# Edge attention on one core: 36 rows a group fetched row by row, by two queues, in place of 8 by one

## The chip, the cores and the metric

The kernel runs on one core of a Trainium2 chip. Times are device microseconds (us) of that core. TensorE (PE) multiplies matrices, VectorE (DVE) and ScalarE (ACT) work on tiles, GpSimd (POOL) and the sync engine (SP) mostly start transfers here. Each engine works through its own list of instructions in order; semaphores tie the lists together. SP and ScalarE can start ordinary DMAs; GpSimd starts gathers, which are DMAs whose source rows are read from a table of indices.

## The reference

The computation is one graph-attention layer with a residual and two norms. There are 12500 nodes of 128 values and 212500 edges, sorted by destination:

```python
Q = (x @ WQ).reshape(N, H, dh); K = (x @ WK)...; V = (x @ WV)...
Eh = (edge_attr @ WE).reshape(-1, H, dh)
score = K[src] * Q[dst] / jnp.sqrt(jnp.float32(dh)) * Eh
score = jnp.exp(jnp.clip(score.sum(-1, keepdims=True), -5.0, 5.0))
msg = V[src] * score
wV = jax.ops.segment_sum(msg, dst, num_segments=N)
Z = jax.ops.segment_sum(score, dst, num_segments=N)
h = x + (wV / (Z + ATTN_EPS)).reshape(N, D)
h = batch_norm(h); out = layer_norm(x + h)
```

H is 8 and dh 16. `K[src]` and `V[src]` are random reads: every edge needs one row of K and V, 256 floats or 1 KB.

## The kernel before, in words

**Table.** First the kernel computes K and V of all nodes and writes them to a table in DRAM, `kvd`, one 1 KB row a node. While the table is being written, GpSimd gathers rows of `x` itself for the first eight groups.

**Groups.** The edges are cut into 1661 tiles of 128 edges, and eight tiles make a group, so that there are 208 groups. For each tile, one gather by GpSimd (line 221) brings 128 rows of `kvd`, one a partition, into a column of the group's slot. Nine slots are used in turn. When VectorE has made the messages of a group (`message`, line 663), its slot is free, and the gathers of the group nine later are queued for GpSimd.

**One group's work.** VectorE multiplies the K rows with the transposed product of Q and edge features (`products`, line 639), sums by head (`scores`, 647), clips (657), and after ScalarE's exp (658, 659) multiplies V with it (`message`, 663). It also builds one-hot matrices (541 to 551) with which TensorE sums the messages by destination (680). ScalarE copies results out of TensorE's accumulators: the edge features (595), the sums (685), the nodes' new values (710), and Q in three bf16 parts, the first of them at line 569 (`q_hi`), the second at 576 (`q_mid`). VectorE computes what remains of Q after the first part at line 573 (`q_rest`), just ahead of `message` in its list.

**Order.** The order on every engine is the order of the calls in the loop over groups, written out by hand. In a pass g it begins: load the edge features of group g + 4 on SP (506; it waits until TensorE is done with the features of group g + 1, since there are three buffers), on some passes load a block of relative destinations on SP (404), then `fetch_rows(g)`, then `q_hi(g + 3)`, `products(g)`, and so on. ScalarE's list around the pass's beginning is thus: `q_mid` of the pass before, then `q_hi`, then the two exps.

**Rows.** In some groups the last of the eight columns is not gathered by GpSimd. Its 128 rows are fetched one at a time by SP: `fetch_rows` (lines 269 to 284) loads the byte offsets of a pass's rows from an SBUF tile (`row_ids`) into registers (274) and starts one DMA of 1 KB for each row (281) into a tile of its own, `byrow`, of which there are two. `row_plan` (61 to 71) decides which groups: eight rows a pass from pass 8 on make a full tile every 16 passes, and it is used two passes after its last row was started (`ROW_LAG`). There are 12 such groups, the first is 25. Before such a column is read, VectorE waits on a semaphore that counts its rows (`rows_there`). A group with such a column splits lines 639, 647 and 663 into two instructions. The offsets' nodes are loaded in pass 2 (`load_row_ids`, 264) and made byte offsets on VectorE in pass 4.

Of the kernel before, what the change touches and what calls it, by code (L numbers as in the profile page):

```python
# [10 lines left out]
U8 = mybir.dt.uint8  # L11
I32 = mybir.dt.int32
# [3 lines left out]
ET = mybir.EngineType  # L16

P = 128
# [4 lines left out]
U = 4  # L23
# [4 lines left out]
EARLY = 3  # L28
RUN = 64
ROWS = P  # L30
FIRST_ROW = 8
LATE = 8
ROW_LAG = 2
SP_ROWS = 8
WORDS = 4
RQ = 4
NSEM = 6
# [40 lines left out]
def gnn_kernel(  # L78
# [31 lines left out]
    consts = ctx.enter_context(tc.tile_pool(name="consts", bufs=1))  # L110
# [129 lines left out]

    by_row, fill = {}, {}
    row_loads = []
    n = SP_ROWS
    row_tiles = row_plan(usizes)
    tot = len(row_tiles) * P
    cols = -(-n // WORDS) * WORDS
    full_rows = tot // n
    blocks = -(-tot // (P * n))
    for q in range(0, full_rows, P):
        row_loads.append((0, q // P * cols, min(P, full_rows - q), n, q * n))  # L250
    if tot % n:
        row_loads.append((full_rows % P, full_rows // P * cols, 1, tot % n, full_rows * n))
    for q in range(-(-tot // n)):
        fill[FIRST_ROW + q] = q
    by_row.update({g: None for g in row_tiles})
    rows_in = [tc.alloc_semaphore(f"rows_in{i}") for i in range(NSEM)]
    row_ids = consts.tile([P, blocks * cols], I32, name="row_ids")
    nc.vector.memset(row_ids, 0)
    kvb = kvd.bitcast(U8).rearrange("n d -> (n d)")

# [1 line left out]
        return [(a, b - 1), (b - 1, b)] if g in by_row and b == G else [(a, b)]  # L262

    def load_row_ids():
        for p, c, m, w, at in row_loads:
            nc.scalar.dma_start(row_ids[p:p + m, c:c + w], bass.AP(
                tensor=rsrc.tensor, offset=rsrc.offset + at, ap=[[n, m], [1, w]]))

    def fetch_rows(g):
        if g not in fill:  # L270
            return
        q = fill[g]
        c = q // P * cols
        _, offs = nc.values_load_multi_w_load_instructions(
            row_ids[q % P:q % P + 1, c:c + cols], engines=(ET.SP,), min_val=0, max_val=(N - 1) * 8 * P,
            skip_runtime_bounds_check_because="node ids")
        for r, off in zip(range(q * n, min(q * n + n, tot)), offs):
# [3 lines left out]
            d = nc.sync.dma_start(by_row[k][r % P:r % P + 1, 0, :].bitcast(U8), kvb[ds(off, 8 * P)].unsqueeze(0))  # L281
# [69 lines left out]
    def within(f, g):  # L351
        return f(g) if 0 <= g < NG else None
# [405 lines left out]
    for q in range(NQ):  # L758
# [13 lines left out]
        k = q - first_step  # L772
# [70 lines left out]
    for g in range(NG - 2):  # L843
        within(load, g + 4)
        within(load_rel, g + 5)
        if (g + 6) % RQ == 0 and (g + 6) // RQ in quads:
            load_quad((g + 6) // RQ)
        fetch_rows(g)
        within(q_hi, g + 3)
        within(products, g)  # L850
        within(q_lo, g + 2)
# [13 lines left out]
        else:  # L865
            left = len(queued)
# [35 lines left out]
        if g == LATE - 2:  # L902
# [3 lines left out]
    g = last - 1  # L906
# [4 lines left out]
                           skip_runtime_bounds_check_because="a count")]  # L911
# [321 lines left out]
```

## Time and profile before

| what | value |
|---|---|
| median of 3 runs | 2134.45 us (2132.48 to 2135.73) |
| profiled execution, its own time | 2128.07 us |
| its span | 2126.3 us |
| PE busy | 1714.8 us (81%) |
| DVE busy | 1591.9 us (75%) |
| POOL busy | 1594.3 us (75%) |
| ACT busy | 671.6 us (32%) |
| gathers from `kvd` | 1585 |
| single rows fetched by SP | 1536 |

Durations come from the profiled execution. The span is the time from its first to its last instruction; the time of a run has 1.8 us more around it. Busy times leave out instructions that only load registers, wait, or start a DMA, so that SP has no busy time at all, and ScalarE's busy time holds no DMA issue.

### The profile page before, as it was taken

How to read it: one execution, taken by the hardware profiler on the slowest of the kernel's cores; microseconds unless marked ns; L12 is line 12 of the kernel's file. 1: busy time of each engine (PE TensorE's matmuls, PEld its weight loads, DVE VectorE, ACT ScalarE, POOL GpSimd, SP SyncE). 2: the span in 40 equal slices, each digit the busy share in tenths (PEclk: the TensorE clock that was granted, in tenths of full speed). 3: DMA queues.
4: the chain of work that ended last, by engine and by line, in shares of the span. 5: the costliest groups of instructions: out<-in, count | busy, mean ns of one | idle time of the engine just before them, and what ended most of it. 6: DMA issues, size and time to landing. Idle time of an engine off the chain costs nothing. (4 is left out here: it accounts for less than half of the span.)

```text
span 2126.3 us, 34575 instructions
## 1 busy us (share of the span) xinstructions
PE 1714.8 (81%) x9414; PEld 1106.1 (52%) x9414; DVE 1591.9 (75%) x3593; ACT 671.6 (32%) x2688; POOL 1594.3 (75%) x1685
## 2 busy tenths in 40 slices
PE   8889999877777777877777778778778777777787
PEld 7566565544444444545444545545445444544456
DVE  4559999777777777777777777777777777777787
ACT  3344343323223223223223223223223232222225
POOL 7777777777777777777777777777777777777775
PEclk9999999998999999998999999888998998988898
DMA  9856666565565565565565565565565565565574
GB/s 311 277 183 206 193 197 195 175 178 171 169 178 169 169 180 167 170 182 169 166 183 164 171 183 168 168 184 167 166 185 165 167 186 165 166 186 165 170 236 126
DMA packets 175392, 386.62 MB, mean 182 GB/s; under 512 B 37518, under 2 KB 91831, under 8 KB 175191
## 3 DMA queue, kind: packets, MB, share of 16 engines
q0 software_dynamic: 78128, 212.05, 33.9%
q1 hardware_dynamic: 92900, 169.50, 25.8%
q10 hardware_dynamic: 4163, 2.78, 0.5%
q8 instruction: 78, 1.28, 0.2%
q14 instruction: 123, 1.01, 0.1%
HBM read 364.57 MB, written 19.63 MB: 181 GB/s over the span
## 5 line engine op out<-in xcount | busy, mean ns | idle before, releaser
L221 POOL DMA_INDIRECT slot<-kvd,srcs x1585 | 1506.0, 950 | 484.0 <-issue 402.8
L639 DVE TENSOR_TENSOR slot<-slot,ps_t 128x512 f32<-128x512 f32 (+1 forms) x410 | 274.7, 678 | 421.2 <-DMA slot<-kvd,srcs 383.8
L621 PE MATMUL ps_t<-ident,wt 128*128 128x128 f32 x1661 | 285.7, 315 | 356.0 <-DVE wt L613 353.0
L680 PE MATMUL ps_a<-msg,oh 128*128 128x136 f32 (+1 forms) x3322 | 526.2, 297 | 1.9 <-DVE msg L663 1.9
L621 PEld LDWEIGHTS ps_t<-ident,wt 128*128 128x128 f32 x1661 | 214.8, 161 | 530.8 <-issue 460.7
L680 PEld LDWEIGHTS ps_a<-msg,oh 128*128 128x128 f32 (+1 forms) x3322 | 426.8, 171 | 81.7 <-issue 54.4
L658 ACT ACTIVATE ps_m<-s 128x64 f32<-128x64 f32 (+1 forms) x209 | 47.5, 227 | 1093.4 <-DVE s L657 1009.4
L588 PE MATMUL ps_e<-ea,w_e 128*128 128x512 f32 x832 | 390.6, 591 | 0.7 <-ACT wt L595 0.7
L613 DVE TENSOR_TENSOR wt<-wt,ps_q 128x512 f32<-128x512 f32 x416 | 264.6, 677 | 2.2 <-PE ps_q L603 2.2
L663 DVE TENSOR_TENSOR msg<-slot,ps_m 128x1024 f32<-128x1024 f32 (+3 forms) x209 | 246.9, 1183 | 0.4 <-ACT ps_m L658 0.3
L647 DVE TENSOR_REDUCE s<-slot 128x64 f32<-128x1024 f32 (+2 forms) x208 | 246.7, 1187 | 0.1
L595 ACT ACTIVATE wt<-ps_e 128x512 f32<-128x512 f32 x416 | 233.4, 618 | 11.5 <-PE ps_e L588 11.2
L603 PE MATMUL ps_q<-ot,q 64*128 64x512 bf16 x1248 | 212.6, 456 | 0.0
L588 PEld LDWEIGHTS ps_e<-ea,w_e 128*128 128x128 f32 x832 | 142.6, 190 | 100.4 <-issue 98.5
L541 DVE TENSOR_TENSOR oh<-ps_m,rel_i 128x512 f32<-128x512 f32 x208 | 142.0, 683 | 11.1 <-PE ps_a L680 11.1
L569 ACT ACTIVATE q<-qs 128x128 bf16<-128x128 f32 x208 | 64.3, 309 | 220.1 <-PE ps_q L603 186.2
L705 PEld LDWEIGHTS ps_a<-ident,at 128*128 128x128 f32 x408 | 71.2, 218 | 111.5 <-issue 55.5
L705 PE MATMUL ps_a<-ident,at 128*128 128x128 f32 x408 | 114.2, 367 | 2.5 <-DVE relrow L395 2.3
L710 ACT ACTIVATE hx<-ps_a 128x64 f32 x408 | 88.3, 217 | 43.1 <-PE ps_a L680 32.1
L530 ACT ACTIVATE xw<-hx 128x64 f32 x416 | 88.1, 279 | 10.4 <-DMA hx<-xT 6.0
L603 PEld LDWEIGHTS <-q 64*128 64x128 bf16 x1248 | 48.9, 103 | 80.7 <-issue 64.1
L561 PE MATMUL ps_a<-w_q,xw 128*128 128x128 f32 x416 | 88.8, 299 | 0.6 <-ACT qs L565 0.4
(180 smaller groups left out, 1633.9 us busy)
## 6 DMA issues: line engine op xcount, KB each, us to landing
ea<-eaT SPq DMA_DIRECT2D x207, 512.0 KB
slot<-kvd,srcs POOLq DMA_INDIRECT x1585
byrow<-kvd SPq DMA_DIRECT2D x1536, 1.0 KB
rbq<-relT SPq DMA_DIRECT2D x94, 256.0 KB
kvd<-slot SPq DMA_DIRECT2D x12, 512.0 KB
kvd<-t SPq DMA_DIRECT2D x12, 512.0 KB
slot<-xT SPq DMA_DIRECT2D x24, 256.0 KB
out<-o SPq DMA_DIRECT2D x23, 256.0 KB
```

Of the source, the lines that this page charges most:

```text
L221: return nc.gpsimd.indirect_dma_start(out=out, out_offset=None, in_=table, in_offset=bass.IndirectOffsetOnAxis(ap=srcs[:, e:e + 1], axis=0))
L541: nc.vector.tensor_tensor(one, iota_ps[:, None, :].to_broadcast([P, n, P]), r[:, :n, None].to_broadcast([P, n, P]), op=OP.is_equal)
L588: nc.tensor.matmul(eh, w_e, EA[g][:, a:b, :].rearrange("p a b -> p (a b)"), start=True, stop=True)
L595: nc.scalar.activation(t[:, :(b - a) * P], EH[g][h], AF.Copy)
L603: nc.tensor.matmul(QE[g][h], Q3[g][r, k, :], OT[g][r, :(b - a) * P], start=(k == 0), stop=(k == 2))
L613: nc.vector.tensor_tensor(t, t, QE[g][h], op=OP.mult)
L621: nc.tensor.transpose(ps[:, j, :], WT[g][h][:, j * P:(j + 1) * P], ident)
L639: step = nc.vector.tensor_tensor(kv, kv, PW[g][i][:, c - a:d - a, :], op=OP.mult)
L647: step = nc.vector.tensor_reduce(SS[g][:, a:b, :], KV[g](a, b, 0).rearrange("p t (h d) -> p t h d", d=DH), axis=AX.X, op=OP.add)
L663: step = nc.vector.tensor_tensor(MSG[g][:, a:b, :P].rearrange("p t (h d) -> p t h d", d=DH), KV[g](a, b, P).rearrange("p t (h d) -> p t h ...
L680: nc.tensor.matmul(AGG[g][WN if j >= n else 0:], OH[g][j], MSG[g][:, j, :], start=(j == 0), stop=(j == n - 1))
L705: nc.tensor.matmul(ps, AT[g], ident, start=True, stop=False)
```

## The change

Each pass now fetches 36 rows in place of 8. SP starts 20 of them and ScalarE starts 16; ScalarE's come in the loop just ahead of `q_hi(g + 3)`. The first fetch is in pass 6 in place of 8. A tile of 128 rows is full every 3.56 passes: 55 groups (11, 15, 18, 22, ..., 203) have a column by rows in place of 12, and GpSimd issues 1542 gathers from `kvd` in place of 1585. The total of single rows is 7040 in place of 1536, over 196 passes (6 to 201).

Each engine loads its own offsets into its own registers: 20 words on SP in place of 8, and 16 words on ScalarE. `row_ids` becomes a tile of 128 x 72 words with two passes in a partition, and it is filled by five DMAs on ScalarE in place of two (two large ones and three for the remainder). Everything else in the loop stays in its place.

```diff
-FIRST_ROW = 8
+FIRST_ROW = 6
-SP_ROWS = 8
+SP_ROWS = 20
+ACT_ROWS = 16
...
-    full, n = sizes.count(U) // 2, SP_ROWS
+    full, n = sizes.count(U) // 2, SP_ROWS + ACT_ROWS
...
+    row_loads.append((0, 0, [[2 * n, pairs], [n, 2], [1, SP_ROWS]], 0, sp_step))
+    row_loads.append((0, act_at, [[2 * n, pairs], [n, 2], [1, ACT_ROWS]], SP_ROWS, act_step))
...
+    def offsets(q, et):
+        c, w, m = (0, sp_step, SP_ROWS) if et == ET.SP else (act_at, act_step, ACT_ROWS)
+        _, offs = nc.values_load_multi_w_load_instructions(
+            row_ids[q // 2:q // 2 + 1, c + q % 2 * w:c + (q % 2 + 1) * w], engines=(et,), min_val=0,
+            max_val=(N - 1) * 8 * P, skip_runtime_bounds_check_because="node ids")
+        return offs[:m]
+
-    def fetch_rows(g):
+    def fetch_rows(g, et, a, b):
         if g not in fill:
             return
-        q = fill[g]
...
+        eng = {ET.SP: nc.sync, ET.Activation: nc.scalar}[et]
+        for r, off in zip(range(at + a, at + b), offsets(fill[g], et)):
             k = row_tiles[r // P]
             if r % P == 0:
                 by_row[k] = rows.tile([P, 1, 2 * P], F32, name="byrow", bufs=2)
-            d = nc.sync.dma_start(by_row[k][r % P:r % P + 1, 0, :].bitcast(U8), kvb[ds(off, 8 * P)].unsqueeze(0))
+            d = eng.dma_start(by_row[k][r % P:r % P + 1, 0, :].bitcast(U8), kvb[ds(off, 8 * P)].unsqueeze(0))
...
-        fetch_rows(g)
+        fetch_rows(g, ET.SP, 0, SP_ROWS)
+        fetch_rows(g, ET.Activation, SP_ROWS, SP_ROWS + ACT_ROWS)
         within(q_hi, g + 3)
```

More of the change, by code (lines that the diff above doesn't have):

```diff
@@ L264, in load_row_ids @@
     def load_row_ids():
[L265 to L269 removed]
+        for p, c, ap, at, step in row_loads:
+            m, k, w = (d[1] for d in ap)
+            nc.scalar.dma_start(
+                row_ids[p:p + m, c:c + k * step].rearrange("p (k w) -> p k w", w=step)[:, :, :w],
+                bass.AP(tensor=rsrc.tensor, offset=rsrc.offset + at, ap=ap))
+    def offsets(q, et):
[5 more added lines that the diff above has]
+    def fetch_rows(g, et, a, b):
         if g not in fill:
             return
[L272 to L277 removed]
+        at = fill[g] * n
+        b = min(b, tot - at)
+        if b <= a:
+            return
+        eng = {ET.SP: nc.sync, ET.Activation: nc.scalar}[et]
+        for r, off in zip(range(at + a, at + b), offsets(fill[g], et)):
             k = row_tiles[r // P]
```

24 lines of the change are left out of this document (15 added, 9 removed).

## The prediction

> **What bounds the kernel now.** I read the groups of costliest instructions first, then the waits of the long middle stretch, then the timeline of GpSimd, and last single groups in the timeline.
>
> ```profile
> L221 POOL DMA_INDIRECT slot<-kvd,srcs x1585 | 1506.0, 950 | 484.0 <-issue 402.8
> DVE slot L639 <- DMA slot<-kvd,srcs: 368.0, 164, 6.2
> ACT ps_m L658 <- DVE s L657: 885.2, 155, 9.3
> SPq L506 <- PE ps_e L588: 913.8, 162, 12.6
> ```
>
> The first row is of the page's groups, the others are of the waits between 380 and 2005 us. GpSimd's gathers take 950 ns each and nearly all of its idle time is "issue", its own gap of 0.3 us before each gather: nobody holds it up. VectorE waits for gathers 164 times there, about once a group, 368 us in all. ScalarE and SP wait long, for VectorE and TensorE: they have room.
>
> ```profile
> 83.25 0.95 POOL L221 DMA_INDIRECT slot<-kvd,srcs  x1 [0.30 <-issue]
> 172.39 0.95 POOL L221 DMA_INDIRECT slot<-kvd,srcs  x1 [0.30 <-issue]
> 174.59 0.94 POOL L221 DMA_INDIRECT slot<-kvd,srcs  x1 [1.25 <-DVE msg L663]
> 2071.94 0.95 POOL L221 DMA_INDIRECT slot<-kvd,srcs  x1 [0.30 <-issue]
> 283.16 0.20 DVE L657 TENSOR_SCALAR s<-s 128x64 f32<-128x64 f32 x1
> 290.54 0.20 DVE L657 TENSOR_SCALAR s<-s 128x64 f32<-128x64 f32 x1
> 1006.34 0.20 DVE L657 TENSOR_SCALAR s<-s 128x64 f32<-128x64 f32 x1
> 1016.34 0.20 DVE L657 TENSOR_SCALAR s<-s 128x64 f32<-128x64 f32 x1
> ```
>
> These are rows of the timeline: the first and last gather from the table, the only gather that waited noticeably, and four clips, one a group. From 174.59 to 2071.94 lie 1512 gathers: 1.255 us each, 10.0 us for a group of eight. VectorE's own pace, while GpSimd is still nine slots ahead, is 7.4 us (283.16 to 290.54); later it is GpSimd's, 10.0 us (1006.34 to 1016.34). So there are three stretches: until 174.59 GpSimd runs ahead until all slots are full, and there its next gather (the 73rd, group 17's first) has to wait for the messages of group 8; then it never stops until 2071.94; then 54.4 us follow to the end of the span. The sum is 1.255 us times the gathers after group 8's messages, and the two ends.
>
> **The change, part by part.** *Gathers removed.* 55 groups with a column by rows in place of 12 take 43 gathers from GpSimd. Two of them (groups 11 and 15) lie before the stop at 174.59, where GpSimd only stops earlier. 41 x 1.255 = 51.5 us come off the long stretch, if no other engine's pass is slower than GpSimd's. That has 8 - 1/3.56 = 7.72 gathers a group now, 9.69 us.
>
> *SP.* Its work is in these rows of the timeline and of the single lines' views (for those: minimum, median and maximum in ns).
>
> ```profile
> 1014.72 0.36 SPq L506 DMA_DIRECT2D ea<-eaT  x1
> 1015.98 2.52 SPq L281 DMA_DIRECT2D byrow<-kvd  x8
> 1026.28 0.36 SPq L506 DMA_DIRECT2D ea<-eaT  x1
> 1026.69 1.24 SPq L404 DMA_DIRECT2D rbq<-relT  x2
> 1029.08 2.57 SPq L281 DMA_DIRECT2D byrow<-kvd  x8
> L274 SPq TENSOR_LOAD <-row_ids x192: 701/735/993, 168.9 to 1992.7; - x192
> L281 SPq DMA_DIRECT2D byrow<-kvd x1536: 221/228/310, 169.9 to 1996.1; - x192
> L910 SPq TENSOR_LOAD <-bad_i x1: 468/468/468, 2064.6 to 2064.6; - x1
> ```
>
> From the features' load to the first row 1.26 us pass (1014.72 to 1015.98), with the eight-word register load of 735 ns in them. Rows follow each other every (2.52 - 0.23) / 7 = 0.327 us, so 20 take 19 x 0.327 + 0.23 = 6.44. Every fourth pass has two loads of relative destinations and reaches its first row after 2.80 us in place of 1.26: 0.39 a pass. Twelve more words in the register load cost between nothing and 12 x 735 / 8 ns = 1.10 us; by the row of the one-word load, 468 ns, seven more words cost 267 ns, and 12 cost 0.46, which I take since it is the same engine and operation. With 0.05 to the next load a pass is 1.26 + 6.44 + 0.39 + 0.46 + 0.05 = 8.6 us (8.1 to 9.2). That is below 9.69, but above VectorE's 7.4.
>
> *ScalarE.* The loads and DMAs are its sequencer's work, in order with the rest.
>
> ```profile
> 1016.57 0.23 ACT L658 ACTIVATE ps_m<-s 128x64 f32<-128x64 f32 x1 [6.57 <-DVE s L657]
> 1018.80 0.34 ACT L576 ACTIVATE q<-qs 128x128 bf16<-128x128 f32 x1
> L523 ACTq TENSOR_LOAD <-base_i x104: 304/308/500, 33.2 to 2026.4; - x104
> L910 ACTq TENSOR_LOAD <-bad_i x1: 289/289/289, 2063.0 to 2063.0; - x1
> ```
>
> From exp to `q_mid` it needs 2.23 us, and then it waited 6.57 for the next exp. Into that wait go the register load of 16 words and 16 rows. One word took 289 ns and four took 308, so 16 are 0.39; the upper bound is 16 x 308 / 4 ns = 1.23. Rows on ScalarE from a register's address are not in this trace; SP's 0.327 is nearest: 15 x 0.327 + 0.23 = 5.14. With 0.06 between, 5.6 us (to 6.4). Its pass is 2.23 + 5.6 + 0.2 for `q_hi` = 8.0 (to 8.9), and again 9.69 hides it. Behind its DMAs wait `q_hi`, then both exps; for them `q_rest` and `message` on VectorE; the latter begins 1.64 us after exp's end (below), so that exp may be that late for nothing.
>
> *Both must keep up over the whole run.* 187 groups (17 to 203) x 9.69 = 1812 us are GpSimd's; SP and ScalarE have 194 passes (8 to 201) for them, so up to 1812 / 194 = 9.3 us a pass they end earlier than GpSimd and cost nothing. Above it each 0.1 us a pass costs 19 us. In the first part of that stretch, where VectorE now goes at 7.4, it will go at SP's 8.6 and catch up with GpSimd later; that costs nothing.
>
> *The stop at 174.59.* Here ScalarE has little room, and the cost is visible.
>
> ```profile
> 161.31 0.30 ACT L576 ACTIVATE q<-qs 128x128 bf16<-128x128 f32 x1
> 163.81 0.20 DVE L657 TENSOR_SCALAR s<-s 128x64 f32<-128x64 f32 x1
> 164.04 0.23 ACT L658 ACTIVATE ps_m<-s 128x64 f32<-128x64 f32 x1 [1.52 <-DVE s L657]
> 165.91 1.28 DVE L663 TENSOR_TENSOR msg<-t,ps_m 128x512 f32<-128x512 f32 x2
> 107.49 0.53 ACTq L266 DMA_DIRECT2D row_ids<-rsrc  x1
> 109.19 0.44 ACTq L172 DMA_DIRECT2D gb<-gamma  x1
> ```
>
> From `q_mid` to exp there are 2.73 us; 5.8 are wanted, so exp is 3.1 late. In pass 6, which still projects K and V of group 7 with ScalarE in the chain, all of it counts; in pass 7 the 1.64 us between exp's end (164.27) and `message` (165.91) come off, 1.5; in pass 8 ScalarE's own ring of 7 us is no longer than VectorE's. Three more DMAs that fill `row_ids` on ScalarE at about 0.5 each (0.53, 0.44) add 1.5. Group 8's messages, and with them group 17's gathers, come 6 us later (0 to 9).
>
> *The rest.* 43 more groups split three VectorE instructions, by these rows:
>
> ```profile
> L639 DVE TENSOR_TENSOR byrow<-byrow,ps_t x12: 279/280/282, 296.0 to 2021.6; 128x128 f32<-128x128 f32 x12
> 172.00:380.00 208.00, 200.47 (x1184) 125.92 (x1183) 204.32 (x465) 82.07 (x337) 156.76 (x166) 0.98 0.66 196
> 380.00:2005.00 1625.00, 1276.40 (x6874) 798.98 (x6875) 1203.95 (x2714) 472.03 (x1966) 1230.37 (x1296) 0.90 0.58 172
> q1 hardware_dynamic: 92900, 169.50, 25.8%
> ```
>
> A piece of 128 x 128 takes 0.28, and saves about half of it on the larger one: some 0.45 us a group for three, in a stretch where VectorE is busy 1203.95 of 1625 us (the third busy time of the window's row). GpSimd's pace covers it; without that cover it would be 19 us. A row's tile is refilled one or two passes after its use, and waits for `message` on SP and ScalarE at most some 2 us in a few passes; SP's room of 1.1 us a pass takes it. The data, 28 KB more by rows and as much less by gathers, is the same.
>
> *Sum.* 2126.3 - 51.5 + 6 = 2080.8 us of span. The profiled execution lies 6.4 us below the median of the runs shown; the same saving of 45.5 us from 2134.45 gives 2089.
>
> **Rivals.** *A, the issues collide (slower).* SP and ScalarE start rows at the same time for 5 of 9 us. If each row paid more than its 0.327, SP's pass would grow first. Break-even with before is (1812 + 45.5) / 194 = 9.57, which is 0.97 above my 8.6, or 0.06 us on each of the 16 rows that overlap. Were issues fully exclusive, each would take 2 x 0.228 = 0.456, 0.13 more: SP's pass 10.7, that is 1.4 x 194 = 270 us over GpSimd's, and the run takes about 2360. Against it:
>
> ```profile
> 85.03 1.08 SPq L417 DMA_DIRECT2D rb<-relT  x2
> 107.30 1.08 SPq L417 DMA_DIRECT2D rb<-relT  x2
> 107.11 0.34 ACTq L266 DMA_DIRECT2D row_ids<-rsrc  x1
> 108.06 0.61 ACTq L170 DMA_DIRECT2D rel_i<-dst  x1
> ```
>
> Two loads on SP took 1.08 us alone at 85.03, and 1.08 at 107.30, while ScalarE started three. [...]
>
> *B, SP's pass is longer than worked out, without collisions*: the register load, or waits for tiles. From 9.3 to 9.57 the gain shrinks from 45 to nothing: 2089 to 2134.
>
> *C, one DMA engine is overloaded.* A packet of SP's queue takes 0.258 x 16 x 2126.3 / 92900 = 0.094 us on average. If all rows ran on one of the 16 engines, 28 more would add 2.6 us in 9.7 to a mean share of 0.58 in the window's row: 0.85, still below one. A gather then lands perhaps 1 us later, once: 2090. Only if rows took 0.15 us each would it bind, and the end be beyond 2134. [...]
>
> **How the numbers follow.** My forecast, GpSimd stays the bound, gets 0.66, with a range of its own of 2080 to 2100 (6 us later or earlier at the stop, and some lag of rows). B gets 0.10, A 0.16, C's binding form and other slower ways 0.08. Within 0.2% (4 us, about what can be told here) falls only a piece of B and A, 0.03. Faster then is 0.66 + 0.08 = 0.74, slower 0.23. The range for 8 in 10 runs from 2078 (no delay at the stop, and 3 us of scatter as among the runs) to 2160, where A costs 0.14 us a pass beyond break-even.
>
> **What would show it.** Right: 1542 gathers from the table at 1.255 us, no idle time of GpSimd but its own after some 181 us, the last one at about 2026; SP's 20 rows in 6.4 us, ScalarE's 16 in 5.1, clips 8.6 apart at first and 9.7 on average later; VectorE still waiting for gathers at line 639. Wrong: GpSimd idle for VectorE's messages in the middle, rows 0.4 us apart, VectorE waiting for exp (line 663 for ScalarE) or for rows, or TensorE for edge features that SP loaded late.

## The result and the profile after

The changed kernel takes 2129.6 us (median of 20 runs, 2121.1 to 2136.0) against 2134.4 us for the kernel before beside it (20 runs): a ratio of 0.9978, 95% interval 0.9969 to 0.9988. It is faster by about 5 us, 0.2%; 2089 was forecast. In five of the seven sets of runs that the experiments were made in, the kernel before itself took 2783 to 2819 us in place of 2130, so a ratio below always stands to the kernel before in its own set.

The profiled execution of the changed kernel has a span of 2130.6 us (before 2126.3) and took 2132.4 us. First the page's groups of GpSimd's gathers and of VectorE's first use of a column by rows (line, engine, operation; count; busy us and mean ns; idle time before it and its main releaser), then two stretches of the run in a table by windows, of after:

```profile
L222 POOL DMA_INDIRECT slot<-kvd,srcs x1542 | 1466.1, 951 | 528.5 <-issue 380.4
L657 DVE TENSOR_TENSOR byrow<-byrow,ps_t 128x128 f32<-128x128 f32 x55 | 15.5, 282 | 122.5 <-DVEq L306 122.5
290.00:1140.00 850.00, 674.02 (x3776) 429.50 (x3772) 663.87 (x1559) 246.80 (x1069) 622.37 (x655) 0.92 0.64 176
1140.00:2000.00 860.00, 685.08 (x3774) 428.14 (x3775) 661.62 (x1542) 252.21 (x1079) 647.84 (x682) 0.93 0.64 177
```

and the same stretches of before:

```profile
290.00:1140.00 850.00, 680.82 (x3731) 423.86 (x3730) 655.75 (x1487) 256.19 (x1068) 643.68 (x678) 0.92 0.59 175
1140.00:2000.00 860.00, 678.53 (x3642) 426.92 (x3642) 632.29 (x1422) 248.39 (x1032) 650.96 (x686) 0.90 0.58 172
```

There are 43 gathers fewer, as forecast, and each still takes 0.95 us. But GpSimd's idle time grew from 484.0 to 528.5 us although it has 43 gaps of 0.3 us fewer. The fifth busy time and count of a window's row, the last ahead of the granted clock, are GpSimd's: between 290 and 1140 us it issued 655 gathers where before it issued 678. VectorE waited 122.5 us for rows at the columns by rows; the 12 such columns of the kernel before had no wait of this kind.

GpSimd's timeline shows the places. The five rows are the gathers behind the three long stops, one of many short ones, and the last gather:

```profile
162.41 0.94 POOL L222 DMA_INDIRECT slot<-kvd,srcs  x1 [10.18 <-DVE s L665]
177.14 0.95 POOL L222 DMA_INDIRECT slot<-kvd,srcs  x1 [6.30 <-issue]
196.83 0.94 POOL L222 DMA_INDIRECT slot<-kvd,srcs  x1 [10.00 <-DVE msg L681]
1004.48 0.94 POOL L222 DMA_INDIRECT slot<-kvd,srcs  x1 [1.39 <-DMA slot<-kvd,srcs]
2076.91 0.95 POOL L222 DMA_INDIRECT slot<-kvd,srcs  x1 [0.30 <-issue]
```

Adding up all that GpSimd idles beyond its own 0.30 us before a gather gives this account of the span:

| term | us |
|---|---|
| 43 gathers x 1.2555 | -54.0 |
| stops between 80 and 290 us: 25.6, before 0.9 | +24.7 |
| stops between 290 and 1140 us: 28.4, before 0 | +28.4 |
| stops between 1140 and 2000 us: 4.4, before 0 | +4.4 |
| first gather 0.35 later; from the last gather to the end 53.7, before 54.4 | -0.3 |
| sum; measured is +4.3 | +3.2 |

So the saving was there in full, and two losses took it back: the **first loss** of about 25 us before 290 us, and the **second loss** of about 28 us after it.

*The first loss* begins on ScalarE. This is its timeline around the loads of `row_ids` in pass 2:

```profile
107.83 1.40 ACTq L276 DMA_DIRECT2D row_ids<-rsrc  x1
109.28 7.51 ACTq L276 DMA_DIRECT2D row_ids<-rsrc  x4
118.95 0.31 ACT L587 ACTIVATE q<-qs 128x128 bf16<-128x128 f32 x1 [10.28 <-DMA row_ids<-rsrc]
119.46 1.06 ACT L340 ACTIVATE xt<-ps_t 128x512 f32<-128x512 f32 x2
126.85 0.35 DVE L714 SCALAR_TENSOR_TENSOR at<-os,keep,rz 128x128 f32<-128x128 f32 x1 [14.26 <-PE ps_a L723]
```

The five loads keep ScalarE from 107.83 to 116.79, 9 us. The two large ones, each with two runs of words in each of 97 partitions, need 1.4 and 4.2 us; the next, of 20 words in one partition, needs 2.7 behind them, and the last two, of the same kind, 0.24 and 0.26. The next instruction of ScalarE, `q_hi` (line 587 here), starts after 10.28 us of idle time, and with it the copies that K and V of group 4 need; the last row, of VectorE, shows the wait that comes of it. From the clip of group 3 to that of group 4 pass 23.9 us, before 14.0. ScalarE's first rows start at 161.4 us, ahead of the exps of group 6; from the clip of group 6 to that of group 7 pass 19.8 us, before 13.2.

*In the second loss* SP hardly waits any more. Its waits between 290 and 1140 us, its longest first, for before and for after, with the loads and rows on SP and ScalarE (minimum, median and maximum in ns) of after:

```profile
SPq L506 <- PE ps_e L588: 463.1, 89, 12.6
```

```profile
SPq L524 <- PE ps_e L606: 3.0, 7, 1.4
L282 SPq TENSOR_LOAD <-row_ids x196: 1382/1448/1801, 161.1 to 2031.0; - x196
L282 ACTq TENSOR_LOAD <-row_ids x195: 1017/1200/1352, 160.2 to 2013.8; - x195
L299 SPq DMA_DIRECT2D byrow<-kvd x3920: 218/228/1982, 162.9 to 2038.9; - x196
L299 ACTq DMA_DIRECT2D byrow<-kvd x3120: 226/232/599, 161.4 to 2020.5; - x195
```

A pass of SP lasts 9.37 us there, of which it works 9.24: rows 6.95, the register load 1.56, edge features 0.42, relative destinations 0.33. 53 of its rows took over 0.3 us to start, up to 1.98, and that excess alone is 30.6 us in this stretch. A tile's rows have landed 6 to 15 us after its last row was issued (12.3 in the mean), where before it was 1.6 to 2.0. And the gathers themselves land late. A gather's landing is taken here as the last event of its semaphore ahead of the gather eight later, which uses the same semaphore and waits for it:

```
kernel          rows/pass  gather lands after, us    extra idle time of GpSimd, us
                           mean    90% (290-1140)    80-290   290-1140   1140-2000
before              8      3.43     5.10               0.9       0.0        0.0
after              36      8.36     9.78              25.6      28.4        4.4
```

Eight gathers are 8 x 1.255 = 10.0 us. With landings of 8.4 us in the mean, the slow ones reach that, and GpSimd stops: of 53 late gathers between 290 and 1140 us, 47 (19.5 of 28.4 us) start 0.26 or 0.76 us after the landing of the gather eight before. The other six, 8.8 us, come at every 106th gather, so at a fixed distance in GpSimd's list; what they wait for is not resolved.

The same events show what part of a gather is late. A gather leaves up to sixteen events on its semaphore (15.5 were recorded in the mean, before 15.8). Of those gathers between 290 and 1140 us of which all sixteen were recorded, the fifteenth comes after 3.49 us in the mean and the last after 8.35; before, after 3.20 and 3.41. So one of a gather's sixteen events, taken here as the landings of sixteen parts, is late, and the others come nearly as they did.

### The profile page after: what moved, and what is told of

The parts are those of the page before. It is cut to its first block, busy times and chain, and to the rows that moved or that the text cites. A ratio compares the mean times of both kernels' runs of the same rounds, so it can differ in the third digit from the quotient of the medians.

```text
span 2130.6 us, 45977 instructions
## 1 busy us (share of the span) xinstructions
PE 1697.0 (80%) x9414; PEld 1100.9 (52%) x9414; DVE 1598.3 (75%) x3722; ACT 650.5 (31%) x2688; POOL 1554.8 (73%) x1642
## 3 DMA queue, kind: packets, MB, share of 16 engines
q1 hardware_dynamic: 97668, 171.95, 28.3%
## 4 chain that ended last, share of the span: by engine, by line
DMA 30%; DVE 15%; PE 14%; issue 11%; SPq 11%; POOL 9%; ACTq 7%; ACT 3%; DVEq 0%; POOLq 0%
DMA slot<-kvd,srcs 21%; POOL slot L222 9%; SPq L299 8%; DMA byrow<-kvd 7%; ACTq L299 5%; PE ps_a L698 3%; DVE s L665 3%; DVE slot L657 2%; SPq L282 2%; PE ps_e L606 2%; DVE msg L681 2%; DVE wt L631 2%; PE ps_t L639 1%; PE ps_t L363 1%; ACTq L282 1%
## 5 line engine op out<-in xcount | busy, mean ns | idle before, releaser
L222 POOL DMA_INDIRECT slot<-kvd,srcs x1542 | 1466.1, 951 | 528.5 <-issue 380.4
L639 PE MATMUL ps_t<-ident,wt 128*128 128x128 f32 x1661 | 265.5, 304 | 281.7 <-DVE wt L631 277.8
L657 DVE TENSOR_TENSOR slot<-slot,ps_t 128x512 f32<-128x512 f32 (+1 forms) x410 | 260.4, 660 | 181.1 <-DMA slot<-kvd,srcs 131.9
L681 DVE TENSOR_TENSOR msg<-slot,ps_m 128x1024 f32<-128x1024 f32 (+3 forms) x209 | 240.8, 1154 | 0.3 <-ACT ps_m L676 0.3
L665 DVE TENSOR_REDUCE s<-slot 128x64 f32<-128x1024 f32 (+2 forms) x208 | 240.4, 1157 | 0.1
L621 PE MATMUL ps_q<-ot,q 64*128 64x512 bf16 x1248 | 198.8, 430 | 0.0
L579 PE MATMUL ps_a<-w_q,xw 128*128 128x128 f32 x416 | 96.0, 315 | 41.6 <-ACT xw L548 41.2
L591 DVE TENSOR_TENSOR qs<-qs,q 128x128 f32<-128x128 f32 x208 | 59.9, 288 | 88.1 <-ACT q L587 83.2
L657 DVE TENSOR_TENSOR byrow<-byrow,ps_t 128x128 f32<-128x128 f32 x55 | 15.5, 282 | 122.5 <-DVEq L306 122.5
L579 PEld LDWEIGHTS ps_a<-w_q,xw 128*128 128x128 f32 x416 | 69.1, 208 | 59.5 <-ACT xw L548 57.7
```

The lines of the kernel that those rows point to most:

```text
L222: return nc.gpsimd.indirect_dma_start(out=out, out_offset=None, in_=table, in_offset=bass.IndirectOffsetOnAxis(ap=srcs[:, e:e + 1], axis=0))
L621: nc.tensor.matmul(QE[g][h], Q3[g][r, k, :], OT[g][r, :(b - a) * P], start=(k == 0), stop=(k == 2))
L639: nc.tensor.transpose(ps[:, j, :], WT[g][h][:, j * P:(j + 1) * P], ident)
L657: step = nc.vector.tensor_tensor(kv, kv, PW[g][i][:, c - a:d - a, :], op=OP.mult)
L665: step = nc.vector.tensor_reduce(SS[g][:, a:b, :], KV[g](a, b, 0).rearrange("p t (h d) -> p t h d", d=DH), axis=AX.X, op=OP.add)
L681: step = nc.vector.tensor_tensor(MSG[g][:, a:b, :P].rearrange("p t (h d) -> p t h d", d=DH), KV[g](a, b, P).rearrange("p t (h d) -> p t h ...
```

## The experiments

What was to be told apart: whether the first loss comes from the loads of `row_ids` or from the early fetches, and whether the second comes from the rows' traffic on one DMA engine (**engine theory**) or from the time SP and ScalarE take to issue (**sequencer theory**).

**1. `row_ids` laid out otherwise** (quick_ids_3). A pass's 36 words lie in one partition, in loads of few large pieces:

```diff
...
-        for p, c, ap, at, step in row_loads:
-            m, k, w = (d[1] for d in ap)
-            nc.scalar.dma_start(
-                row_ids[p:p + m, c:c + k * step].rearrange("p (k w) -> p k w", w=step)[:, :, :w],
-                bass.AP(tensor=rsrc.tensor, offset=rsrc.offset + at, ap=ap))
+        for p, c, m, w, at in row_loads:
+            nc.scalar.dma_start(row_ids[p:p + m, c:c + w], bass.AP(
+                tensor=rsrc.tensor, offset=rsrc.offset + at, ap=[[n, m], [1, w]]))
...
```

> Only the layout of row_ids differs from the changed kernel: 36 words of one pass lie in one partition's row, filled by loads of 128, 64 and fewer partitions in place of two of 97. If this chip runs the kernel before in about 2134 us: by the early-loss theory ScalarE leaves the loads after about 3 us in place of 9, group 4's period falls from 23.9 towards 14 us, and 10 to 18 us of GpSimd's 25 us of extra idle time before 290 us go, a ratio to the kernel before of 0.990 to 0.993. Rival: the fetches in passes 6 and 7 make the early loss, and less than 5 us go. Neither changes the 28 us between 290 and 1140 us. If the chip runs the kernel before in about 2785 us, as in the runs with 1.13, the ratio is 1.13 again, and the early part tells nothing new.

Measured: 2121.72 us against 2130.13, a ratio of 0.9966 (0.9949 to 0.9984). ScalarE's timeline in this kernel:

```profile
107.05 0.34 ACTq L270 DMA_DIRECT2D row_ids<-rsrc  x1
107.43 0.55 ACTq L270 DMA_DIRECT2D row_ids<-rsrc  x1
108.01 1.10 ACTq L270 DMA_DIRECT2D row_ids<-rsrc  x2
```

The loads are done after 2.1 us in place of 9. GpSimd's extra idle time before 290 us falls from 25.6 to 18.4 us, that is by 7, between what the two theories said: the loads make a part of the first loss, and the larger part has another cause. The second loss stays (25.4 us). The events show how the loads differ: those of 128 and 64 partitions leave sixteen on their semaphores, that of 3 partitions four, and each of the changed kernel's two large ones only two, like a single row.

**2. First fetch in pass 10** (start_ten_2): the kernel of 1 with

```diff
-FIRST_ROW = 6
+FIRST_ROW = 10
```

> quick_ids (36 rows a pass) with the first fetch in pass 10 in place of 6, so that no row is fetched before GpSimd has begun to run freely; 42 gathers fewer than the kernel before. Where the kernel before takes about 2134 us: if the fetches of passes 6 to 9 make the 18 us of extra idle time that quick_ids still has before 290 us, under 4 us of it stay and the time falls by 12 to 16 us against quick_ids less 1.3 us for the gather that comes back, to a ratio of 0.990 or less; if that idle time has another cause, 10 us or more of it stay. The 25 us between 290 and 1140 us stay in both. Where the kernel before takes about 2800 us: 1.13 again.

Measured: 2104.76 us against 2130.23, 0.9877 (0.9861 to 0.9894). Before 290 us 5.9 us are left. So the fetches of passes 6 to 9, ahead of the point where GpSimd has filled its slots, make 12 us of the first loss (about 1 us of it can come from the loads of `row_ids`, two here in place of four). Under 4 us were expected to be left; for the 5 us above the 0.9 of the kernel before no cause is shown. After 290 us the loss stays (22.6 us).

**3. Fewer rows** (rows_20_again, and with the later start rows_28_ten_2), both with the layout of 1:

```diff
-SP_ROWS = 20
-ACT_ROWS = 16
+SP_ROWS = 12
+ACT_ROWS = 8
```

```diff
-FIRST_ROW = 6
+FIRST_ROW = 10
-SP_ROWS = 20
-ACT_ROWS = 16
+SP_ROWS = 16
+ACT_ROWS = 12
```

> quick_ids with 20 rows a pass in place of 36, 19 gathers fewer than the kernel before in place of 43, -24 us. If this chip runs the kernel before in about 2134 us: the one-engine theory and the sequencer theory expect rows to land within 4 us of their tile's last issue in place of 10 to 15, GpSimd's extra idle time between 290 and 1140 us to fall from 28 to under 5 us, and a time of 2105 to 2115 us, a ratio of 0.986 to 0.991. Rival: the 28 us have nothing to do with the rows' rate, 15 us or more of them stay, and the ratio is 0.994 or more. On a chip of 2785 us the ratio is 1.01 again.

> 28 rows a pass (16 by SP, 12 by ScalarE), first fetch in pass 10, row_ids with a pass in one partition's row: some 42 tiles by rows, 30 gathers fewer than the kernel before, -37 us. Where the kernel before takes about 2134 us: the one-engine theory expects 0 to 10 us of GpSimd's extra idle time after 290 us (none at 20 rows, 25 to 28 us at 36) and under 4 us before 290 us, a time of 2095 to 2110 us, a ratio of 0.983 to 0.991. Rival: the loss grows straight with the rows above 20, 12 to 14 us stay, and the ratio is 0.99 or more. Where the kernel before takes about 2800 us: 1.07 again.

Measured: with 20 rows 2116.42 us against 2130.13, 0.9944 (0.9928 to 0.9961); with 28 rows 2097.68 against 2130.23, **0.9846** (0.9829 to 0.9862), the fastest of all versions, 33 us under the kernel before. In neither does GpSimd idle beyond its own gap after 290 us. With 20 rows the time was nevertheless 5 us over the expected range and the ratio where the rival put it: 6.9 us of stops before 290 us stay, since this kernel still fetches from pass 6 on, and a gather's slot is 1.2578 us long in place of 1.2549, 4.5 us in all. Rows of rows_28_ten_2: the one stop that is left, GpSimd's longest waits between 290 and 1140 us (all of 0.3 us now), SP's longest there, and VectorE's at the columns by rows:

```profile
177.14 0.94 POOL L222 DMA_INDIRECT slot<-kvd,srcs  x1 [5.00 <-DVE msg L675]
POOL slot L222 <- issue: 163.8, 537, 0.3
POOL slot L222 <- DMA slot<-kvd,srcs: 13.1, 43, 0.3
SPq L518 <- PE ps_e L600: 170.5, 48, 8.3
L651 DVE TENSOR_TENSOR byrow<-byrow,ps_t 128x128 f32<-128x128 f32 x42 | 11.8, 280 | 0.0
```

For after, the two waits of GpSimd were:

```profile
POOL slot L222 <- issue: 156.4, 492, 2.2
POOL slot L222 <- DMA slot<-kvd,srcs: 28.3, 71, 1.4
```

The last number of a row is the longest wait: 2.2 and 1.4 us after, 0.3 with 28 rows. The second loss does not grow straight with the rows: it is nothing at 28 and 23 to 28 us at 36, so it sets in between. The span of the 28 rows is accounted for: 30 gathers x 1.2555 = -37.7, the stop at 177 us +3.8 over before's, a gather's own slot 1.2578 in place of 1.2549 us, +4.6, and 2.0 less behind the last gather: -31.3, as measured.

**4. The same bytes in twice as many transfers** (rows_20_in_two_3): the kernel with 20 rows, each row in two halves:

```diff
-            d = eng.dma_start(by_row[k][r % P:r % P + 1, 0, :].bitcast(U8), kvb[ds(off, 8 * P)].unsqueeze(0))
-            d.then_inc(rows_in[r // P % NSEM], 16)
+            for u in (0, 4 * P):
+                d = eng.dma_start(by_row[k][r % P:r % P + 1, 0, u // 4:u // 4 + P].bitcast(U8),
+                                  kvb[ds(off + u, 4 * P)].unsqueeze(0))
+                d.then_inc(rows_in[r // P % NSEM], 16)
...
-        w = nc.vector.wait_ge(rows_in[k % NSEM], 16 * P * (k // NSEM + 1))
+        w = nc.vector.wait_ge(rows_in[k % NSEM], 32 * P * (k // NSEM + 1))
```

> rows_20 with each row as two transfers of 512 bytes: the same gathers and bytes, 40 row transfers a pass, 24 by SP. Where the kernel before takes about 2134 us: if the bytes on one DMA engine make the loss, rows land 2 to 5 us after their tile's last issue, GpSimd does not idle after 290 us, and the ratio is 0.993 to 0.997. If each transfer has a price at that engine whatever its bytes, rows land 10 us late or later and GpSimd idles 20 us or more between 290 and 1140 us. If the sequencers decide, SP's pass of 9.7 us lies a little over 9.57, rows land within 5 us of their issue, and GpSimd idles 0 to 0.5 us a pass in all parts of the run alike. Where the kernel before takes about 2800 us: 1.26 again.

Measured: 2400.4 us against 2130.23, 1.1275 (1.1256 to 1.1294). The first rows are SP's timeline, then VectorE's wait for rows and GpSimd's longest waits, between 290 and 1140 us:

```profile
1003.59 0.36 SPq L520 DMA_DIRECT2D ea<-eaT  x1
1005.07 9.05 SPq L294 DMA_DIRECT2D byrow<-kvd  x24
1014.23 0.37 SPq L520 DMA_DIRECT2D ea<-eaT  x1
1015.73 7.21 SPq L294 DMA_DIRECT2D byrow<-kvd  x20
DVE byrow L653 <- DVEq L302: 139.6, 12, 15.1
POOL slot L222 <- DVE byrow L653: 71.6, 10, 10.9
POOL slot L222 <- DMA slot<-kvd,srcs: 7.9, 26, 0.3
```

SP's pass is 10.64 us from one load of edge features to the next (1003.59 to 1014.23), 10.9 in the mean with 0.1 of waits: here SP is the bound, and every engine goes at its pace in all parts of the run. It is 1.2 us longer than expected, 1.0 of it for working out the halves' addresses in registers. Yet rows land 1 to 6 us after their tile's last issue, and no gather waits for one of its own kind (0.3 us at most in the last row). The same table as above:

```
kernel              rows/pass      gather lands after, us    extra idle time of GpSimd, us
                                   mean    90% (290-1140)    80-290   290-1140   1140-2000
rows_20_again       20             3.89     5.68               6.9       0.0        0.0
rows_28_ten_2       28             4.05     5.68               4.7       0.0        0.0
quick_ids_3         36             8.17     9.72              18.4      25.4        2.9
start_ten_2         36             8.25     9.77               5.9      22.6        2.7
rows_20_in_two_3    40 of 512 B    4.73     6.10              17.8      75.7       87.8
```

So rows cost in two ways here, told apart by what GpSimd waited for. Where SP's pass was too long (this run, 10.9 us), VectorE waited for rows (139.6 us between 290 and 1140 us) and GpSimd for VectorE (71.6 us). Where 36 rows a pass came (after, 1 and 2), gathers landed late (8.2 to 8.4 us in the mean) and GpSimd waited for gathers (28.3 us in after). The run does not part bytes from transfers: its halves carry 20 KB in 10.9 us and its gathers land after 4.73 us, whole rows carry 28 KB in 9.3 us and they land after 4.05, so each transfer seems to have a price too; and with SP as the bound all traffic is less here (a DMA share of 0.56 between 290 and 1140 us, with 28 rows 0.61, in after 0.64).

What speaks for the engine theory is again the last event of a gather, of those gathers between 290 and 1140 us with all sixteen recorded. The fifteenth comes after 3.3 to 3.5 us in all of these kernels. The sixteenth comes after 3.87 us with 20 rows, 4.06 with 28, 4.73 with 40 halves, and 8.26 to 8.35 with 36: the lateness is in one part of sixteen alone and comes with the rows. Why a slow issue on SP or ScalarE should pick out one part of a gather that GpSimd starts, no run shows.

**5. The rows' bytes halved, the issues kept** (half_rows, half_rows_2), meant to settle it: the kernel of 2 without the second half of each such row, the values, so that its output is not the reference's:

```diff
...
-            d = eng.dma_start(by_row[k][r % P:r % P + 1, 0, :].bitcast(U8), kvb[ds(off, 8 * P)].unsqueeze(0))
+            d = eng.dma_start(by_row[k][r % P:r % P + 1, 0, :].bitcast(U8), kvb[ds(off, 4 * P)].unsqueeze(0))
```

> start_ten with only the first 512 of each row's 1024 bytes fetched, by the same 36 transfers a pass: SP and ScalarE issue as many transfers as before, the one DMA engine carries half the bytes. The second half of a row fetched this way, the values, is left out, and the product over the first half stands in its place, so the output is not the reference's; VectorE does the same work. Engine theory: the queue of that engine makes the second loss: rows land within 4 us of their tile's last issue in place of 12, SP's transfers are not held back (28 us of excess in 52 of them go), SP's work a pass falls from 9.26 to about 8.9 us, and of GpSimd's 22.6 us of extra idle time between 290 and 1140 us under 6 stay; the time is 17 to 25 us under start_ten's, a ratio of 0.976 to 0.980. Sequencer theory: SP's own instructions, 9.26 us a pass against some 9.1 that GpSimd's gathers need in that stretch, make it, and 17 us or more stay, a ratio of 0.985 to 0.988. By both 3 us or less are lost after 1140 us, where the gathers need 9.6 us a pass.

> start_ten with only the first 512 of each row's 1024 bytes fetched, by the same 36 transfers a pass; the second half of such a row, the values, is left out, and the product over the first half stands in its place, so the output is not the reference's; VectorE does the same work. Where the kernel before takes about 2130 us: by the engine theory rows land within 4 us of their tile's last issue in place of 12, SP's work a pass falls from 9.26 to about 8.9 us, under 6 of the 22.6 us of GpSimd's extra idle time between 290 and 1140 us stay, and the ratio is 0.976 to 0.980. By the sequencer theory 17 us or more stay, a ratio of 0.985 to 0.988. Where the kernel before takes about 2800 us: 1.13 again, which tells nothing of this.

Both times the kernel before took 2.8 ms beside it (2818.9 and 2813.4), and the ratios are 1.1346 (1.1310 to 1.1381) and 1.1302 (1.1226 to 1.1378), as with whole rows there (1.1309). GpSimd waits there for VectorE's messages and for rows (212.3 and 83.8 us between 290 and 1140 us in half_rows_2) and hardly for gathers (0.6 us), so the loss in question does not arise, and the run tells nothing of it. Beside half_rows ran 32 rows (16 and 16, first fetch in pass 10):

> 32 rows a pass, 16 by SP and 16 by ScalarE, first fetch in pass 10, row_ids with a pass in one partition's row: some 47 tiles by rows, 35 or 36 gathers fewer than the kernel before, -45 us. SP has 16 rows as in rows_28_ten, where its work was 7.3 us a pass with 2.0 us of waits; ScalarE has 16 as in start_ten. Sequencer theory: SP decides at 20 rows and not at 16, so nothing is lost after 290 us, and the time is 2088 to 2094 us, a ratio of 0.980 to 0.983. Engine theory: 32 rows of 0.073 us beside 0.58 of other traffic make 0.82 of one engine, between 0.79 (nothing lost) and 0.85 (25 us): rows land 4 to 10 us late and 3 to 15 us are lost, a ratio of 0.982 to 0.989.

Measured there: 2919.05 against 2818.9, 1.0353 (1.0324 to 1.0382); neither theory's number applies, and 32 rows stay untried where the kernel before takes 2130 us.

**6. A row in two or four pieces** (two_engines, four_engines), meant to bring more DMA engines to a row. The changed kernel with a row written as two pieces of 512 bytes, or four of 256, by one transfer, with a gap between the pieces in the tile:

```diff
...
-                by_row[k] = rows.tile([P, 1, 2 * P], F32, name="byrow", bufs=2)
-            d = eng.dma_start(by_row[k][r % P:r % P + 1, 0, :].bitcast(U8), kvb[ds(off, 8 * P)].unsqueeze(0))
+                by_row[k] = rows.tile([P, 2, P + 16], F32, name="byrow", bufs=2)
+            d = eng.dma_start(by_row[k][r % P:r % P + 1, :, :P].bitcast(U8),
+                              kvb[ds(off, 8 * P)].rearrange("(a b) -> a b", a=2).unsqueeze(0))
```

> [...] Theory E: rows land 6 to 9 us after their last issue in place of 12 to 15 between 290 and 1140 us, GpSimd's idle beyond its own 0.3 us falls from 28 us there to 10 to 18, and the run is 10 to 18 us faster than the changed kernel: 2112 to 2120. Theory S: issue is no shorter, so landing, stalls and time stay (2128 to 2135), or get worse if two pieces take longer to issue.

> [...] Theory E: rows land 3 to 6 us after their last issue, the stalls in the middle fall to 3 to 10 us, and the run is 18 to 25 us faster than the changed kernel: 2105 to 2112. Theory S: no faster than the changed kernel (2128 to 2140), slower if four pieces cost more issue time.

Measured where the kernel before took 2785.91: 4502.96 (1.6156, 1.6122 to 1.6190) and 4542.07 (1.6302, 1.6260 to 1.6345). A row takes SP 552 ns to issue in the mean with two pieces and 564 with four, where beside them one piece took 243 (quick_ids). Such a row costs SP more than twice the time, with two pieces as with four, and that covers whatever else the pieces may change. That a row in pieces goes to more engines was the author's assumption; no run shows it, and the times given for theory E (the engine theory) rest on it. It was not tried where the kernel before takes 2130 us.

**7. The same kernels where the kernel before takes 2.8 ms.** The changed kernel and those of 1 to 4 also ran there:

> The changed kernel with the load of the row numbers laid out as before it: one pass's 36 words in a partition, loaded as 128, 64, 3 and 1 partitions, in place of two loads of 97 partitions x 2 pieces. In the changed kernel ScalarE spent 9 us (107.8 to 116.8) on issuing these loads, and group 4 came 10 us later. Theory E (all single rows run on one DMA engine, whose queue then delays rows and gathers) and theory S (SP's and ScalarE's issue time is what delays) expect the same here: 4 issues of about 0.5 us, group 4's period 14 to 15 us in place of 23.9, GpSimd's early stops 16 us in all in place of 25.6, and the end 8 to 10 us earlier: 2120. If the early delay were hidden by GpSimd's lead, no change.

> The same, and rows from pass 10 on in place of 6 (54 tiles, 1543 gathers), so that no row is fetched before group 8's messages have released GpSimd's first full stop. Both theories: early stops of GpSimd 1 to 4 us in place of 25.6 (in the kernel before 0.9), the stalls in the middle as in the changed kernel (28 us by either theory), and 20 to 24 us less than the changed kernel: 2106 to 2110. If passes 6 and 7 are not what costs the other 16 us, it stays near quick_ids.

> The changed kernel itself, beside the three that follow, so that they are compared on the same chip. From its first profile both theories expect a ratio to the kernel before of 0.996 to 1.000 (measured 0.9978), with 25 us of GpSimd's idle time between 80 and 290 us and 28 us between 290 and 1140 us beyond its own 0.3 us a gather.

> Only the layout of row_ids differs from the changed kernel: 36 words of one pass lie in one partition's row, filled by loads of 128, 64 and fewer partitions in place of two of 97. Early-loss theory: the loads leave ScalarE in about 3 us in place of 9, group 4's period falls from 23.9 towards 14 us, and of GpSimd's 25 us of extra idle time before 290 us 10 to 18 go; the time falls by as much against the changed kernel, a ratio to the kernel before of 0.990 to 0.993. Rival: the fetches in passes 6 and 7, not the loads, make the early loss, and then less than 5 us go. Neither says that the 28 us after 290 us change.

> quick_ids with 12 rows a pass by SP and 8 by ScalarE in place of 20 and 16: some 31 tiles are fetched by rows in place of 55, so about 19 gathers fewer than before in place of 43, -24 us. One-engine theory: the rows' share of one DMA engine falls from about 0.27 to 0.15, rows land within 4 us of their tile's last issue in place of 10 to 15, and GpSimd's extra idle time between 290 and 1140 us falls from 28 to under 5 us. Sequencer theory: SP's pass falls from 8.9 to about 5.7 us, and the 28 us go as well. Rival: the 28 us have nothing to do with the rows' rate, and 15 us or more of them stay. By the first two the time is 20 to 30 us under that of before, a ratio of 0.986 to 0.991.

> rows_20 with each row fetched by two transfers of 512 bytes in place of one of 1024: the same gathers, the same bytes, 40 row transfers a pass (24 by SP, 16 by ScalarE). If the bytes on one DMA engine make the loss, it stays as in rows_20, and its time within 5 us. If each transfer has a price of its own at that engine, whatever its bytes, the loss is that of the changed kernel or more: rows land 10 us late or later and GpSimd idles 28 us or more between 290 and 1140 us. If the sequencers make it, SP's pass is 0.4 + 1.0 + 24 x 0.33 + 0.4 = 9.7 us, just over the 9.57 at which SP decides, and GpSimd loses 0 to 0.5 us a pass, up to 100 us over all 200 passes, in all parts of the run alike.

> rows_20 with 28 rows a pass (16 by SP, 12 by ScalarE) and the first fetch in pass 10 in place of 6: some 42 tiles by rows, 30 gathers fewer than the kernel before, -37 us. One-engine theory: 28 rows of 0.073 us take 0.21 of one engine's time beside some 0.58 of other traffic, between the 0.73 of 20 rows (no extra idle time after 290 us) and the 0.85 of 36 (25 to 28 us): 0 to 10 us of idle time stay, and with the fetches behind GpSimd's stop under 4 us before 290 us. Time 2095 to 2110 us, a ratio of 0.983 to 0.991. Sequencer theory: SP's pass is 7.5 us, under 9.57, and nothing stays. Rival: the loss grows straight with the rows above 20, then 12 to 14 us stay, and the ratio is 0.99 or more.

> rows_20 with each row fetched by two transfers of 512 bytes in place of one of 1024: the same gathers and bytes, 40 row transfers a pass, 24 of them by SP. On a chip that runs the kernel before in about 2134 us: if the bytes on one DMA engine make the loss, rows land 2 to 5 us after their tile's last issue as in rows_20, GpSimd does not idle after 290 us, and the time is within 6 us of that of rows_20 (a ratio of 0.993 to 0.997). If each transfer has a price at that engine whatever its bytes, rows land 10 us late or later and GpSimd idles 20 us or more between 290 and 1140 us. If the sequencers decide, SP's pass is 0.4 + 1.0 + 24 x 0.33 + 0.4 = 9.7 us, a little over 9.57, rows still land within 5 us of their issue, and GpSimd idles 0 to 0.5 us a pass in all parts of the run alike, up to 100 us.

| kernel | us, before | ratio (95%) |
|---|---|---|
| quick_ids | 3159.44, 2785.91 | 1.1346 (1.1320 to 1.1371) |
| start_ten | 3149.93, 2785.91 | 1.1309 (1.1285 to 1.1333) |
| the changed kernel (after_beside) | 3159.25, 2783.24 | 1.1343 (1.1303 to 1.1383) |
| quick_ids_again | 3161.33, 2783.24 | 1.1367 (1.1337 to 1.1396) |
| rows_20 | 2810.56, 2783.24 | 1.0112 (1.0086 to 1.0139) |
| rows_20_in_two | 3483.33, 2783.24 | 1.2535 (1.2501 to 1.2570) |
| rows_28_ten | 3010.05, 2804.26 | 1.0748 (1.0696 to 1.0800) |
| rows_20_in_two_again | 3554.19, 2804.26 | 1.2678 (1.2637 to 1.2719) |

No expectation in times of 2.1 ms could hold here. What decides in these runs is told in the last section; there rows take longer to start, and none of the versions tried beats the kernel before.

## Why the prediction was wrong, by its steps

*Gathers removed* was right: 1542 gathers at the same 1.255 us, and 54 us in the whole run that went. *GpSimd stays the bound* was right as well; with 28 rows a pass the 30 gathers saved come out as time but for a few us (run 3). What failed are two terms that were priced as small.

*The stop at 174.59*, +6 us (0 to 9): measured +24.7. Three more DMAs at "about 0.5 each" was the wrong row: the loads that the change widens were priced by one of a few words a partition, but in the changed form one alone takes 4.2 us to issue, and the five take 9 (run 1: 2.1 us in another layout, 7 us of idle time less). Most of the rest lies in the fetches of passes 6 to 9, counted as 3.1 + 1.5 us: run 2 shows 12. The remaining 5 us are open. ScalarE's register load of 16 words was taken at 0.39 us and is 1.20 (the upper bound, 1.23, was the right end), and the delay was followed through exp alone, not through ScalarE's copies for K and V of the next groups, which TensorE and then VectorE wait for.

*Rival C*, one DMA engine overloaded: "A gather then lands perhaps 1 us later, once: 2090. Only if rows took 0.15 us each would it bind." This is the sentence that failed. The engine's share of 0.85, an estimate (no run shows the share of a single engine), was added up as if a share below one cost nothing. It also counted the 28 new rows alone: by the prediction's own 0.094 us, 36 rows in 9.4 us are 0.36 and the share some 0.93, while 28 rows in 9.3 us make 0.86 (both estimates). So the step describes the kernel with 28 rows, whose gathers do land 0.6 us later and stop nothing. With 36 the gathers land 5 us later in the mean, and as GpSimd's gathers use eight semaphores in turn, it stops whenever the one eight earlier is not there after 10 us. Rows need not take 0.15 us for that. The loss lies between 290 and 1140 us, where the passes still catch up with GpSimd's lead (9.37 us a pass against 9.60 later) and gathers land after 8.36 us, against 7.56 later; that the faster passes are the reason for this is argued, not shown.

In the trace each row is 1 x 1 element of 1 KB, and 1152 rows left 2,258 to 2,281 DMA events on their semaphore, two each, while a gather leaves some 15.5 that were recorded. That a row goes to one engine fits these numbers; the trace does not name an engine. So it is shown that one of a gather's sixteen parts is late when 36 rows a pass are fetched, and that this makes 47 of the 53 late gathers; that it is the part on an engine which carries all the rows is the author's reading, which fits all of this. Run 5 was to test that directly and could not.

*SP's pass*, 8.6 us (8.1 to 9.2): 9.24 of work in that stretch, just over the range, and 8.87 later. Rows are 0.32 us apart as taken. The register load was taken 0.46 us longer than that of eight words and is 0.71 longer; another 0.34 us a pass are the 53 rows that took over 0.3 us to start, which 20 and 28 rows a pass hardly show (none and two). It stayed below the 9.69 of GpSimd's eight gathers, so by itself it costs nothing, as the step said. Run 4 shows what it costs when it does not: 10.9 us a pass, and 270 us over the kernel before.

*ScalarE's pass*, 8.0 us (to 8.9): 8.2 from the rows of one pass to those of the next (1001.69 to 1009.85), and hidden, but for the passes around the stop.

*Rival A*, the issues collide: not in this run. Rows are 0.32 us apart on both, and the median row takes SP 228 ns whether ScalarE is starting one at that time or not; so none paid for another. The marks of the forecast were half right: 1542 gathers and the rows' pace came; the absence of idle time after 181 us, the last gather at 2026 (it was 2076.9) and VectorE waiting mainly for gathers at the products (between 290 and 1140 us it waits for rows) did not.

## What to carry to other kernels

When work is moved from a bound engine to another route, add up the resource that both routes share, here by the reading above one of the DMA engines, and ask how late it may deliver before the bound engine stops. Here eight gathers in flight gave 10.0 us; with landings of 8.4 us in the mean the late ones reached that and cost 19.5 us between 290 and 1140 us, at an estimated share of 0.93. Look by the amount for the point where it sets in: with the same layout and start, 28 rows a pass gained 33 us and 36 gained 25. And price what a change does in the first passes by the rows of those passes, each instruction in its form: here the stops before 290 us cost 24.7 us, where 6 had been priced.

## What the hardware showed that was not expected

**A register load took longer with each word**: on SP 735 ns for 8 words, 967 for 12, 1199 for 16 and 1448 for 20 (medians; the kernel before, those with 20 and with 28 rows, after), that is 58 to 62 ns for each further word. The step from one word to eight (468 to 735 ns, 38 a word) was no guide to it. ScalarE: 962 for 12 (28 rows) and 1200 for 16 (after).

**Two pieces in a transfer of one row** took SP 552 ns to issue in the mean, where one took 243 (run 6).

**A load of 97 partitions, in two pieces each, left as few events as a single row.** There were two on its semaphore, where loads of 128 and 64 partitions left sixteen and one of 3 partitions four (run 1), and a load of 20 words behind it took ScalarE 2.7 us in place of 0.25.

**Rows were held up while gathers were issued.** In run 7, many of SP's and ScalarE's instructions came to a pace of one in 0.70 us while GpSimd's gathers were being issued. From the changed kernel there: SP's rows with minimum, median and maximum in ns, then SP's and GpSimd's timelines:

```profile
L299 SPq MOVE byrow<-kvd x3920: 2/29/1395, 225.2 to 3078.6; - x196
L299 SPq DMA_DIRECT2D byrow<-kvd x3920: 3/228/1394, 225.3 to 3078.7; - x196
1000.53 11.53 SPq L299 DMA_DIRECT2D byrow<-kvd  x20
1004.16 0.95 POOL L222 DMA_INDIRECT slot<-kvd,srcs  x1 [0.30 <-issue]
1009.21 0.94 POOL L222 DMA_INDIRECT slot<-kvd,srcs  x1 [4.11 <-DVE msg L681]
```

Twenty rows take 11.53 us in place of 6.8, and even the register move ahead of a row, at most 38 ns in the result's profile, takes up to 1395. While a gather is on GpSimd, the mean step within a pass from one instruction of the rows to the next (steps under 1.6 us) is 407 ns on SP, 35% of them over 600; between gathers it is 234. In the result's profile it is 166 and 165. This is not quite rival A, since the moves start no DMA and it goes with GpSimd's gathers; what makes some sets of runs show it is open (one chip showed both: the kernel before took 2130.23 us on it and 2813.43 in a later set). Whoever relies on the gain of 28 rows should know that it turned into a loss of 7% there.
